# A first node pass with k and v only, beside the edge tables; q and skip inside the steps; no zero fills

## The chip, the cores and the metric

One core of a Trainium2 chip runs the whole kernel. The time is device microseconds of one launch. It is given as the median of several runs; the trace is of one further, profiled execution.

## The reference

The graph has 12500 nodes of 128 features (`x`) and 200000 edges. The edges are sorted by destination `dst`; the sources `src` are random. The destinations are not spread evenly: low node numbers have many more edges than high ones. Two residual blocks follow each other, each with a layer norm and a ReLU in front:

```
h = max(layernorm(x), 0)
x = x + conv2(conv1(h))              # two attention layers
h = max(layernorm(x), 0)
x = x + tensor_product_scatter(h)    # returned

conv(x):                             # 4 heads x 32
    q, k, v = x@Wq+bq, x@Wk+bk, x@Wv+bv
    e = edge_weight * We
    alpha = sum_c(q[dst] * (k[src]+e)) / sqrt(32)
    p = exp(alpha - segment_max(alpha, dst)[dst])
    w = p / segment_sum(p, dst)[dst]
    return segment_sum((v[src]+e) * w, dst) + x@Ws + bs

tensor_product_scatter(x):           # 32 scalars and 32 vectors a node
    s = tensor_product(x[src], edge_attr_9, w0..w4)
    return segment_sum(s, dst) / sqrt(10)
```

The term `x@Ws + bs` is called skip below.

## The kernel before

The nodes are cut into 98 windows of 128 nodes, the edges into 1563 tiles of 128, four tiles to a group: 391 groups. An edge that has a group's first destination plus 0 to 127 as its destination is a one of a 128x128 matrix (`O`, `one_hot`, L719), so that TensorE can bring a node's row to its edges and sum edges into their nodes.

*Edge tables* (`gnn_kernel`, from L1175). `dst`, `src` and `edge_weight` are loaded with one tile to a row and turned by TensorE, so that a tile becomes a column. Many small DMAs with strides fetch the first and last destination of the tiles and groups. A `flag` says whether the list meets the assumptions on its order (it does for this input); the program then branches on it (L1296) into `sorted_path`, else into `general_path`, which never runs here.

*Sorted path: tables and zero fills* (L556 to about L645). `REL` is each edge's destination relative to its group's first, `SEL` and `PEN` handle nodes that lie in two groups, `b_int` holds the groups' first nodes, the weights are joined to `WA` (q, an edge column per head, k, v: 388 columns). ScalarE's DMA queue writes zeros to all of `sum_d` (two tensors, named `fsum` in the trace) and `out_d` (`fout`) in DRAM.

*First node pass* (L690 to 705). 14 iterations of seven windows: load x, statistics on DVE, normalise with ReLU on ACT, and per window a transpose, a product of 388 columns (L667), its eviction on DVE (L668), a product of 128 columns for skip (L672) and its eviction (L701). SyncE's queue stores q (`fq`), k and v (`fkv`) and skip (`fs`).

*The two attention layers* (`conv`, L846 on). The loop's order is written by hand (`manual_schedule`), and it is straight-line code. Step s does, among others: SyncE fetches the 128 rows of q of group s+4 (`fetch_q`, L864) from a row that it reads from `b_int` into a register with a bounds check; GpSimd (POOL) issues four indirect gathers for group s+3 (`fetch_kv`, L725), 128 rows of 1 KB each; TensorE brings q to the edges (`query`, L885), DVE makes the scores (L932 to 935); for group m = s - 12, DVE makes the messages (L895, L896), TensorE sums them (`sum_up`, L915, L917), ACT evicts the sums (L920) and SyncE stores them (L923). Once in eight groups, a batch's running maximum is found by scans (L952, L955, L982). The lag of 12 groups is the reason why k and v of 16 groups are held (`bufs=LAG + 4`).

When a window's last group is summed (`window_steps`), the node work of the window follows in the later steps: `nodes_between` in layer 0 (mean, transpose, skip, residual, product with the next layer's `WA`, eviction L786, three stores) and `nodes_mixed` in layer 1 (second layer norm and a product with 352 columns). Windows 96 and 97 fall after the last group, at different steps, so one is worked on after the other.

*Scatter* (`load`, `sums`, L1115 on). Gathers of 1408-byte rows (`hg`, eight groups held), products with the edge numbers on ACT and DVE, sums on TensorE (L1147), eviction (L1150), store (L1151), and `nodes_out` adds the residual and writes the output. Only SyncE's order is by hand here; for the other engines the framework's scheduler decides.

Of the kernel before, what the change touches and what calls it, by code (L numbers as in the profile page):

```python
# [18 lines left out]
U = 4  # L19
UNROLL = 4  # L20
# [6 lines left out]
def general_path(ctx: ExitStack, tc: tile.TileContext, x, src, dst, edge_attr, edge_weight, conv1, conv2, tpw, out,  # L27
# [38 lines left out]
    X = cpool.tile([P, NW, D], F32, name="X")  # L66
# [284 lines left out]
    with tc.tile_pool(name="nrm2", bufs=1) as np_:  # L351
        layernorm_pass(np_.tile([P, NW, 2], F32, name="nrm2"), second)

# [10 lines left out]
    with ExitStack() as st:  # L364
# [5 lines left out]
        with tc.tile_pool(name="aprep", bufs=2) as ap_:  # L370
            d2 = ap_.tile([P, TP], F32, name="d2", bufs=1)
            d4 = ap_.tile([P, TP], F32, name="d4", bufs=1)
            for g in range(NG):
# [10 lines left out]
                for j0 in range(0, 9, 4):  # L384
                    n = min(4, 9 - j0)
                    pt = psum.tile([P, 4, P], F32, name="qd", bufs=2)
                    for j in range(j0, j0 + n):
                        nc.tensor.transpose(pt[:, j - j0, :], rows[:, :, j], ident)
                    if j0 == 0:
                        nc.scalar.copy(ea[:, 0:4, c], pt)  # L390
                    for j in range(j0, j0 + n):
                        if j in tmap:
                            for k in tmap[j]:
                                nc.vector.tensor_copy(ea[:, 4 + k, c], pt[:, j - j0, :])
                        elif j == 6:
                            nc.scalar.copy(d2[:, c], pt[:, j - j0, :])
                        elif j == 8:
                            nc.scalar.copy(d4[:, c], pt[:, j - j0, :])

            nc.vector.tensor_scalar(ea[:, 8, :], d2, 2.0 * r3, None, op0=OP.mult)  # L400
            nc.vector.tensor_scalar(d2, d2, -r3, None, op0=OP.mult)
            nc.vector.tensor_sub(ea[:, 4, :], d2, d4)
            nc.vector.tensor_add(ea[:, 12, :], d2, d4)
# [65 lines left out]
        with tc.For_i(0, NW, 1) as w:  # L469
# [11 lines left out]
            wi = X[:, ds(w, 1), :].rearrange("p a b -> p (a b)")  # L481
            nc.vector.tensor_add(wi, wi, py)

    nc.sync.dma_start(out[0:half * P, :].rearrange("(w p) d -> p w d", p=P), X[:, 0:half, :])
    nc.scalar.dma_start(out[half * P:(NW - 1) * P, :].rearrange("(w p) d -> p w d", p=P), X[:, half:NW - 1, :])
    nc.sync.dma_start(out[(NW - 1) * P:N, :], X[0:LASTN, NW - 1, :])
# [7 lines left out]
def window_steps(nw, ngr):  # L494


    return [math.ceil(ngr * math.sqrt((w + 1) / nw)) + 3 for w in range(nw)]


def sorted_path(ctx: ExitStack, tc: tile.TileContext, x, src, dst, edge_attr, edge_weight, conv1, conv2, tpw, out,  # L500
                srcI, dstF, ewF, FG, LG, seg_d):
# [7 lines left out]
    E = src.shape[0]  # L509
# [10 lines left out]
    KW = 7  # L520
    GE = U * P
    LF = seg_d.shape[1]
    SQ = 2 * BG + 1
    assert NW % KW == 0 and D == P
    scale = 1.0 / math.sqrt(C)
    r3, r10, avg = math.sqrt(1.0 / 3.0), math.sqrt(0.1), 1.0 / math.sqrt(10.0)
    n0, n1 = math.sqrt(1.0 / 64.0), math.sqrt(3.0 / 96.0)
    AHEAD = 4
    CHAIN = 4
# [4 lines left out]
    batch = lambda j: list(range(starts[j], starts[j] + sizes[j]))  # L534
    batch_of = [j for j in range(NB) for _ in range(sizes[j])]
    take = {}
    for w, g in enumerate(window_steps(NW, NGR)):
        take.setdefault(g, []).append(w)
    MIX = 352

    dram = ctx.enter_context(tc.tile_pool(name="fdram", bufs=1, space=bass.MemoryType.DRAM))
    kv_d = [dram.tile([NW * P, 2 * D], F32, name=f"fkv{i}") for i in range(2)]
    q_d = [dram.tile([NW * P + P, QD], F32, name=f"fq{i}") for i in range(2)]
    s1_d = dram.tile([NW * P, D], F32, name="fs1")
# [5 lines left out]
    rows_of = lambda t, a: t[a * P:(a + KW) * P, :].rearrange("(w p) c -> p w c", p=P)  # L550

    cp = ctx.enter_context(tc.tile_pool(name="fconst", bufs=1))
    ident = cp.tile([P, P], F32, name="fident")
    make_identity(nc, ident)
    ones = cp.tile([1, P], F32, name="fones")
    nc.vector.memset(ones, 1.0)  # L556
    eps = cp.tile([P, 1], F32, name="feps")
    nc.vector.memset(eps, EPS)


    REL = cp.tile([P, NGR, U], F32, name="fREL")
    nc.vector.tensor_sub(REL, dstF[:, 0:NGR * U].rearrange("p (g u) -> p g u", u=U),
                         FG[:, :, None].to_broadcast([P, NGR, U]))
    b_int = cp.tile([1, NGR], I32, name="fb")
    nc.vector.tensor_copy(b_int, FG[0:1, :])
    pidx = cp.tile([P, 1], F32, name="fpidx")
    nc.gpsimd.iota(pidx, pattern=[[0, 1]], base=0, channel_multiplier=1, allow_small_or_imprecise_dtypes=True)
    SEL = cp.tile([P, NGR], F32, name="fSEL")
    nc.vector.memset(SEL[:, 0:1], 0.0)
    nc.vector.tensor_sub(SEL[:, 1:NGR], FG[:, 1:NGR], FG[:, 0:NGR - 1])  # L570
    nc.vector.tensor_scalar(SEL[:, 1:NGR], SEL[:, 1:NGR], pidx, None, op0=OP.is_equal)

    PEN = cp.tile([1, NB, SQ], F32, name="fPEN")
    nc.vector.memset(PEN, -BIG)
    with tc.tile_pool(name="fpen", bufs=1) as pp:
        v = pp.tile([1, NGR, 2], F32, name="pf")
        nc.vector.memset(v, -BIG)
        nc.vector.tensor_sub(v[:, 1:NGR, 0], LG[0:1, 0:NGR - 1], FG[0:1, 1:NGR])
        nc.vector.tensor_scalar(v[:, 1:NGR, 0], v[:, 1:NGR, 0], BIG, None, op0=OP.mult)
        nc.vector.tensor_sub(v[:, 0:NGR, 1], FG[0:1, :], LG[0:1, :])  # L580
        nc.vector.tensor_scalar(v[:, 0:NGR, 1], v[:, 0:NGR, 1], BIG, None, op0=OP.mult)
        even = sizes.count(BG)
        nc.vector.tensor_copy(PEN[:, 0:even, 1:SQ], v[:, 0:even * BG, :].rearrange("o (b g) j -> o b (g j)", g=BG))
        for j in range(even, NB):
            n = sizes[j]
            nc.vector.tensor_copy(PEN[:, j, 1:1 + 2 * n], v[:, starts[j]:starts[j] + n, :].rearrange("o g j -> o (g j)"))

    EW = cp.tile([P, NGR * U, 2], F32, name="fEW")
    nc.vector.memset(EW[:, :, 0:1], 1.0)
    nc.vector.tensor_copy(EW[:, :, 1], ewF[:, 0:NGR * U])  # L590


    WA, BA, WS, BS, WE = [], [], [], [], []
    row = lambda b_: bass.AP(tensor=b_.tensor, offset=b_.offset, ap=[[0, P], [1, D]])
    wm = cp.tile([P, MIX], F32, name="fwm")
    with tc.tile_pool(name="fprep", bufs=1) as wp:
        zero = wp.tile([P, KW * SW], F32, name="zero")
        nc.vector.memset(zero, 0.0)
        for i in range(2):
            nc.scalar.dma_start(q_d[i][NW * P:NW * P + P, :], zero[:, 0:QD])  # L600
        for a in range(0, NW, KW):
            for i in range(2):
                nc.scalar.dma_start(rows_of(sum_d[i], a), zero.rearrange("p (w c) -> p w c", c=SW))
            nc.scalar.dma_start(rows_of(out_d, a), zero[:, 0:KW * D].rearrange("p (w c) -> p w c", c=D))
        for li, (Wq, bq, Wk, bk, Wv, bv, We, Ws, bs) in enumerate((conv1, conv2)):
            wa = cp.tile([P, AW], F32, name=f"fWA{li}")
            ba = cp.tile([P, AW], F32, name=f"fBA{li}")
            ws = cp.tile([P, D], F32, name=f"fWS{li}")
            bst = cp.tile([P, D], F32, name=f"fBS{li}")
            we = cp.tile([P, D], F32, name=f"fWE{li}")  # L610
            nc.sync.dma_start(we, row(We))
            for c0, w_, b_ in ((0, Wq, bq), (QD, Wk, bk), (QD + D, Wv, bv)):
                nc.sync.dma_start(wa[:, c0:c0 + D], w_)
                nc.sync.dma_start(ba[:, c0:c0 + D], row(b_))
            nc.sync.dma_start(ws, Ws)
            nc.sync.dma_start(bst, row(bs))
            for t in (wa, ba):
                nc.vector.tensor_scalar(t[:, 0:D], t[:, 0:D], scale, None, op0=OP.mult)
                tm = wp.tile([P, D], F32, name="tmw", bufs=2)
                nc.vector.tensor_mul(tm, t[:, 0:D], we)  # L620
                nc.vector.tensor_reduce(t[:, D:QD], tm.rearrange("p (h c) -> p h c", h=H), AX.X, OP.add)
            WA.append(wa)
            BA.append(ba)
            WS.append(ws)
            BS.append(bst)
            WE.append(we)

        w0 = wp.tile([32, 2, 32], F32, name="w0")
        nc.vector.memset(wm, 0.0)
        for j, (k, c0, f) in enumerate(((0, 0, n0), (1, 128, n1 * r3))):  # L630
            nc.sync.dma_start(w0[:, j, :], tpw[k].rearrange("u o w -> u (o w)"))
            nc.vector.tensor_scalar(wm[0:32, c0:c0 + 32], w0[:, j, :], f * avg, None, op0=OP.mult)
        w1 = wp.tile([P, 3, 3, 32], F32, name="w1")
        nc.vector.memset(w1, 0.0)
        for i in range(3):
            for k in range(3):
# [701 lines left out]
```

## Time and profile before

| | |
|---|---|
| median of 14 runs | 9321.29 us (9276.72 to 9351.28) |
| the profiled execution | 9316.81 us |
| its span, first to last instruction | 9315.0 us |
| mean granted TensorE clock | 0.764 |
| busy: PE / DVE / POOL / ACT | 63 / 54 / 48 / 19% |
| head, until the first gather | 0 to 272 us |
| attention layer 0 | 272 to 3263 us |
| attention layer 1 | 3263 to 6213 us |
| scatter and output | 6213 to 9315 us |

The span lies 1.8 us under the execution's own time. The busy times are averages over stages that are limited by different things, so each stage is to be read alone. In the rows below, a group of instructions is given as line, engine, operation, output<-input by the names in the program, shape, count, then busy time, the mean in ns of one, and the idle time of the engine just before them with what ended it. "remote" and "issue" are waits whose end the trace can't tie to an instruction, and in which nothing shown was waited for.

### The profile page before, as it was taken

The page shows a single profiled execution, that of the slowest core. Times are in us where ns is not written, and L with a number is a line of the kernel's source. Part 1 is how long each engine was busy: PE and PEld are TensorE (multiplying, and loading weights), DVE is VectorE, ACT ScalarE, POOL GpSimd, SP SyncE. Part 2 cuts the span into 40 slices and gives each one's busy share as a digit, 9 for nine tenths or more (in the row PEclk, how much of TensorE's full clock was granted, in tenths as well). Part 3 has the DMA queues.
Part 4 walks back from the last instruction along what each step waited for, and adds up shares of the span by engine and source line. Part 5 has one row for each costly group of instructions (what it writes and reads, how often), then busy time and mean ns, then how long its engine had stood idle before and what let it go on. Part 6 is the DMA issues. An engine that isn't in the chain of part 4 may idle for free.

```text
span 9315.0 us, 113271 instructions
## 1 busy us (share of the span) xinstructions
PE 5826.4 (63%) x33627; PEld 4837.3 (52%) x33628; DVE 5004.0 (54%) x11883; ACT 1751.6 (19%) x5162; POOL 4479.4 (48%) x4729
## 2 busy tenths in 40 slices
PE   4456666666666645666666666656767666666766
PEld 2344545545544434445444545436666556555666
DVE  5345555555555634555555555655555555554555
ACT  2111111111111111122222222221112111111111
POOL 0455555555454355555555545535444445444543
PEclk7677777777777767777777777868878778887778
DMA  7333333334344333333333334434344434433443
GB/s 217 110 95 100 103 106 107 109 109 115 107 115 116 101 91 96 100 103 106 106 103 108 107 109 113 120 101 111 106 107 109 110 105 114 109 106 106 116 113 95
DMA packets 838118, 1019.90 MB, mean 109 GB/s; under 512 B 138151, under 2 KB 651377, under 8 KB 837492
## 3 DMA queue, kind: packets, MB, share of 16 engines
q0 software_dynamic: 250240, 692.16, 27.1%
q1 hardware_dynamic: 545233, 300.14, 11.3%
q10 hardware_dynamic: 42019, 20.26, 0.8%
q8 instruction: 270, 4.42, 0.2%
q14 instruction: 356, 2.92, 0.1%
HBM read 826.93 MB, written 185.10 MB: 109 GB/s over the span
## 4 chain that ended last, share of the span: by engine, by line
PE 25%; another core or an unknown queue 18%; DVE 8%; issue 7%; ACT 3%; DMA 2%; POOL 1%; SPq 0%; DVEq 0%; ACTq 0%; POOLq 0%
PE pa L1147 13%; PE pa L917 4%; PE pq L885 2%; PE po L906 2%; ACT M L1125 1%; DVE O L719 1%; POOL kv L725 1%; PE pa L915 1%; DVE msg L895 1%; PE pa L1144 1%; DVE prod L932 1%; DVE top L952 1%; DVE tops L955 1%; DVE AL L935 1%
## 5 line engine op out<-in xcount | busy, mean ns | idle before, releaser
L725 POOL DMA_INDIRECT kv<-fkv,srcI x3128 | 2989.8, 956 | 2870.8 <-issue 813.6
L1147 PE MATMUL pa<-M,O 128*128 128x128 f32 (+1 forms) x12512 | 1926.1, 316 | 993.2 <-ACT acc L1150 759.2
L1147 PEld LDWEIGHTS pa<-M,O 128*128 128x128 f32 x12512 | 1784.6, 227 | 1148.6 <-ACT acc L1150 795.7
L725 POOL DMA_INDIRECT hg<-fhm,srcI x1564 | 1482.5, 948 | 1644.5 <-issue 1388.3
L906 PE MATMUL po<-fident,O 128*128 128x128 f32 x3128 | 677.3, 356 | 1316.8 <-DVE O L719 1075.0
L885 PE MATMUL pq<-qw,OT 128*128 128x132 f32 x6256 | 1091.6, 330 | 645.1 <-ACT OT L908 379.3
L917 PE MATMUL pa<-msg,O 128*128 128x136 f32 x6256 | 1433.3, 367 | 13.6 <-DVE msg L896 6.5
L885 PEld LDWEIGHTS pq<-qw,OT 128*128 128x128 f32 x6256 | 1007.4, 238 | 752.4 <-ACT OT L908 521.0
L917 PEld LDWEIGHTS pa<-msg,O 128*128 128x128 f32 x6256 | 1161.1, 256 | 288.1 <-issue 275.4
L906 PEld LDWEIGHTS po<-fident,O 128*128 128x128 f32 x3128 | 460.5, 180 | 1428.6 <-issue 819.3
L719 DVE TENSOR_TENSOR O<-iob,fREL 128x512 f32<-128x512 f32 x1173 | 799.7, 682 | 686.7 <-remote 414.3
L908 ACT COPY OT<-po 128x512 f32<-128x512 f32 x782 | 458.2, 586 | 2501.8 <-PE po L906 931.9
L932 DVE TENSOR_TENSOR prod<-pq,kv 128x512 f32<-128x512 f32 x782 | 534.3, 683 | 697.4 <-remote 287.9
L895 DVE TENSOR_TENSOR msg<-kv,wb 128x512 f32<-128x512 f32 x782 | 527.6, 675 | 276.1 <-ACT cfb L1004 224.7
L1150 ACT COPY acc<-pa 128x128 f32<-128x128 f32 x391 | 104.1, 266 | 2460.1 <-remote 1235.2
L935 DVE TENSOR_REDUCE AL<-prod 128x16 f32<-128x528 f32 x782 | 549.6, 703 | 26.8
L920 ACT COPY acc<-pa 128x136 f32<-128x136 f32 x782 | 213.6, 273 | 1593.1 <-PE pa L917 607.7
L1125 ACT ACTIVATE M<-hg,s 128x128 f32<-128x128 f32 x1564 | 505.8, 394 | 9.2 <-DMA hg<-fhm,srcI 7.9
L1129 DVE TENSOR_TENSOR M<-hg,sh 128x384 f32<-128x384 f32 x391 | 214.2, 548 | 455.9 <-remote 380.9
L1140 DVE TENSOR_TENSOR M<-M,tm 128x384 f32<-128x384 f32 x782 | 426.2, 545 | 0.2
L1139 DVE TENSOR_TENSOR tm<-hg,sh 128x384 f32<-128x384 f32 x782 | 405.8, 565 | 0.0
L915 PE MATMUL pa<-acc,fSEL 128*1 128x136 f32 x1368 | 334.7, 335 | 0.0
(184 smaller groups left out, 4236.4 us busy)
## 6 DMA issues: line engine op xcount, KB each, us to landing
fsum<-acc SPq DMA_DIRECT2D x782, 68.0 KB
qw<-fq SPq DMA_DIRECT2D x782, 66.0 KB
kv<-fkv,srcI POOLq DMA_INDIRECT x3128
hg<-fhm,srcI POOLq DMA_INDIRECT x1564
fout<-acc SPq DMA_DIRECT2D x391, 64.0 KB
fhm<-qkv SPq DMA_DIRECT2D x98, 176.0 KB
fsum<-zero ACTq DMA_DIRECT2D x28, 476.0 KB
A<-fsum SPq DMA_DIRECT2D x196, 68.0 KB
```

Source lines behind the costliest of these rows:

```text
L719: nc.vector.tensor_tensor(O, iob[:, None, :].to_broadcast([P, U, P]), REL[:, g, :, None].to_broadcast([P, U, P]), op=OP.is_equal)
L725: nc.gpsimd.indirect_dma_start(out=t[:, u, :], out_offset=None, in_=rows[:, :], in_offset=bass.IndirectOffsetOnAxis(ap=srcI[:, g * U + u:g ...
L885: nc.tensor.matmul(pqs[g][:, u, 0:QD], OT[:, u, :], qw, start=True, stop=True)
L895: nc.vector.tensor_mul(msg[:, :, :, 0:C], kv4(kv, D), pp[:, :, i, :, None].to_broadcast([P, U, H, C]))
L906: nc.tensor.transpose(po[:, u, :], Os[g][:, u, :], ident)
L908: nc.scalar.copy(OTs[g], po)
L915: nc.tensor.matmul(pa[0:1, :], SEL[:, g:g + 1], accs.pop(g - 1).rearrange("p h c -> p (h c)"), start=False, stop=False)
L917: nc.tensor.matmul(pa, O[:, u, :], msg[:, u].rearrange("p h c -> p (h c)"), start=(u == 0), stop=(u == U - 1))
L932: nc.vector.tensor_mul(prod[:, :, :, 0:C], pq[:, :, 0:D].rearrange("p u (h c) -> p u h c", h=H), kv4(kvs[g], 0))
L935: nc.vector.tensor_reduce(ALs[j][:, :, i, :], prod, AX.X, OP.add)
L1125: nc.scalar.activation(M[:, u, 0, :], hg[:, u, 0:P], AF.Copy, scale=s0[:, i * U + u:i * U + u + 1])
L1147: nc.tensor.matmul(pa[:, 0:n], O[:, u, :], M[:, u, c, 0:n], start=(u == 0 and c == 0), stop=(u == U - 1 and c == 2))
```

## The change

1. The first and last destinations of the groups come from TensorE (products with a selection matrix `pick` and with the identity) in place of the small strided DMAs. Casts go in blocks of four tiles, `REL` is made straight from PSUM, and the checks behind `flag` take fewer operations.
2. The zero fills go, except for the last window of the two `sum_d`. `window_steps` is clamped to the last group.
3. The first node pass moves ahead of the branch. It makes only k and v, from seven windows at a time. The normalisation is split: POOL subtracts the mean from all seven windows at once, ACT takes ReLU behind the transposes, and the factor 1/std goes into the evictions, four of them on DVE and three on ACT, with POOL adding the bias to the latter. The factors of all windows stay in `RS`. q and skip are made here for the first seven windows only.
4. Small table work (a list `beside`: `SEL`, `PEN`, weights, iota and so on) is put on POOL in between, some five pieces per iteration.
5. In layer 0, `nodes_asked` makes q and skip of the other 91 windows in the steps, two windows a batch, ahead of their use.
6. `bases` reads both row numbers of a step at once, from a table of pairs, without a bounds check.
7. The windows left at the last group are worked on at once, each in its own half of an idle `pq` bank, and the loop has three steps less.
8. More buffers: kv 16 -> 18 groups, hg and O in the scatter 8 -> 14, A, s1 and mv 2 -> 4, xt 4 -> 5, qkv, y and hT 2 -> 3. The scores' transpose tile `aT` shares one PSUM bank, `ab`, with the new asks.

`general_path` is changed too, but does not run.

```diff
-    return [math.ceil(ngr * math.sqrt((w + 1) / nw)) + 3 for w in range(nw)]
+    return [min(math.ceil(ngr * math.sqrt((w + 1) / nw)) + SLACK, ngr) for w in range(nw)]
+def query_steps(nw, ngr):
+    sizes, out, e = batch_sizes(ngr), [], -1
+    for n in sizes:
+        e += n
+        out += [e + 6, e + 8]
+    return {KW + k: s for k, s in enumerate(out[:nw - KW])}
...
-        for a in range(0, NW, KW):
-            for i in range(2):
-                nc.scalar.dma_start(rows_of(sum_d[i], a), zero.rearrange("p (w c) -> p w c", c=SW))
-            nc.scalar.dma_start(rows_of(out_d, a), zero[:, 0:KW * D].rearrange("p (w c) -> p w c", c=D))
+    for i in range(2):
+        nc.scalar.dma_start(window(sum_d[i], NW - 1), sh_.zero)
...
-    def base_of(g):
-        return nc.values_load(b_int[0:1, g:g + 1], engines=[SPE], min_val=0, max_val=N - 1)
+    def bases(*where):
+        _, v = nc.values_load_multi_w_load_instructions(
+            sh_.bases[0:1, where[0]:where[-1] + 1], engines=[SPE], min_val=0, max_val=N - 1,
+            skip_runtime_bounds_check_because=...)
+        return v
...
+    def nodes_asked(pool, nd, w):
+        st = {}
+        def load():
+            st["x"] = pool.tile([P, D], F32, name="xq", bufs=2)
+            load_x(st["x"], w)
+        def turn():
+            st["h"] = pool.tile([P, D], F32, name="hq", bufs=2)
+            nc.scalar.activation(st["h"], st["x"], AF.Relu, bias=sh_.RS[:, w, 1:2], scale=sh_.RS[:, w, 0:1])
+            nc.tensor.transpose(nd[:, 0:P], st["h"], ident)
+            st["hT"] = pool.tile([P, P], F32, name="hqT", bufs=2)
+            nc.scalar.copy(st["hT"], nd[:, 0:P])
+        def project():
+            nc.tensor.matmul(nd[:, 0:QD + D], st["hT"], sh_.WQ, start=True, stop=True)
+        def evict():
+            st["q"] = pool.tile([P, QD + D], F32, name="qs", bufs=2)
+            nc.vector.tensor_add(st["q"], nd[:, 0:QD + D], sh_.BQ)
+        def store():
+            nc.sync.dma_start(window(q_d[0], w), st["q"][:, 0:QD])
+            nc.sync.dma_start(window(s1_d, w), st["q"][:, QD:QD + D])
+        return [(-6, "load", load), (-2, "late", turn), (-1, "early", project), (-1, "late", evict), (0, "store", store)]
...
-            kvs[g] = pool.tile([P, U, 2 * D], F32, name="kv", bufs=LAG + 4)
+            kvs[g] = pool.tile([P, U, 2 * D], F32, name="kv", bufs=LAG + 6)
...
-            hg = pool.tile([P, U, MIX], F32, name="hg", bufs=8)
+            hg = pool.tile([P, U, MIX], F32, name="hg", bufs=14)
...
+                if m == NGR:
+                    spare = ps.tile([P, U, 256], F32, name="pq").rearrange("p (w u) c -> p w (u c)", w=2)
+                for k, w in enumerate(take.get(m, [])):
+                    for d, place, f in nodes(pool, nd if m < NGR else spare[:, k, :], w):
                         plan.setdefault((s + d, place), []).append(f)
-                if 0 <= m - 1 < NGR:
-                    store_sums(m - 1)
-                if 0 <= s + AHEAD < NGR:
-                    fetch_q(s + AHEAD)
+                run(s, "store")
+                q, r = s + AHEAD, m - 1
+                if 0 <= q < NGR and 0 <= r < NGR:
+                    bq, br = bases(2 * q, 2 * q + 1)
...
+                if 0 <= r < NGR:
+                    store_sums(r, br)
+                if 0 <= q < NGR:
+                    fetch_q(q, bq)
```

The new first node pass, in `gnn_kernel` ahead of the branch:

```diff
+        def normalized(a):
+            if a + 2 * KW < NW:
+                xs[a + 2 * KW] = load_x(a + 2 * KW)
+            xt = xs.pop(a)
...
+            for w in range(KW):
+                nc.vector.bn_stats(st[:, w, :], xt[:, w, :])
+                nc.vector.bn_aggr(mv[:, w, :], st[:, w, :])
+            nc.gpsimd.tensor_sub(xt, xt, mv[:, :, 0:1].to_broadcast([P, KW, D]))
+            rs = RS[:, a:a + KW, :]
+            nc.scalar.activation(rs[:, :, 0], mv[:, :, 1], AF.Sqrt, bias=eps)
+            nc.vector.reciprocal(rs[:, :, 0], rs[:, :, 0])
+            nc.vector.scalar_tensor_tensor(rs[:, :, 1], mv[:, :, 0], -1.0, rs[:, :, 0], op0=OP.mult, op1=OP.mult)
+            hT = npool.tile([P, KW, P], F32, name="hT", bufs=2) if a else hT0
+            for b, n in ((0, 4), (4, 3)):
+                pt = ps.tile([P, 4, P], F32, name="pt")
+                for k in range(n):
+                    nc.tensor.transpose(pt[:, k, :], xt[:, b + k, :], ident)
+                nc.scalar.activation(whole(hT[:, b:b + n, :]), whole(pt[:, 0:n, :]), AF.Relu)
+            return hT
+        def keys(a, hT):
+            kv = npool.tile([P, KW, 2 * D], F32, name="kvn", bufs=2)
+            for w in range(KW):
+                r = RS[:, a + w, 0:1]
+                pj = ps.tile([P, 2 * D], F32, name="pj", bufs=3)
+                nc.tensor.matmul(pj, hT[:, w, :], WKV, start=True, stop=True)
+                if w % 2:
+                    nc.scalar.activation(kv[:, w, :], pj, AF.Copy, scale=r)
+                else:
+                    nc.vector.scalar_tensor_tensor(kv[:, w, :], pj, r, BKV, op0=OP.mult, op1=OP.add)
+            nc.gpsimd.tensor_add(kv[:, 1:KW:2, :], kv[:, 1:KW:2, :], BKV[:, None, :].to_broadcast([P, KW // 2, 2 * D]))
+            nc.sync.dma_start(rows_of(kv_d[0], a), kv)
...
+            for a in range(0, NW + KW, KW):
+                hN = normalized(a) if a < NW else None
+                for f in beside[0:each]:
+                    f()
+                del beside[0:each]
+                if a:
+                    keys(a - KW, hT)
+                hT = hN
```

## The prediction

> **What bounds the kernel now.** I first cut the trace into its stages (boundaries read off the timeline: the first gather at 272, the next layer's first gather at 3263, the scatter's first work at 6213) and asked for each engine's busy time in them. Columns: stretch, length, busy us (instructions) of PE, PEld, DVE, ACT, POOL, then granted clock, DMA share, GB/s.
>
> ```profile
> core 0: us, PE busy (x) PEld busy (x) DVE busy (x) ACT busy (x) POOL busy (x), PEclk, DMA share, GB/s
> 60.00:130.00 70.00, 0.00 (x0) 0.00 (x0) 1.35 (x8) 1.28 (x1) 0.00 (x0) 0.50 0.96 274
> 130.00:272.00 142.00, 112.14 (x490) 72.61 (x490) 105.40 (x438) 64.66 (x210) 0.25 (x1) 0.94 0.75 222
> 272.00:3263.00 2991.00, 1828.26 (x9776) 1452.57 (x9776) 1616.48 (x3917) 423.94 (x1224) 1498.63 (x1564) 0.75 0.38 106
> 3263.00:6213.00 2950.00, 1788.81 (x9580) 1431.70 (x9580) 1606.12 (x4012) 669.94 (x1622) 1491.19 (x1564) 0.74 0.37 104
> 6213.00:9315.00 3102.00, 2086.73 (x13733) 1872.53 (x13733) 1639.45 (x3374) 577.09 (x2053) 1482.55 (x1564) 0.80 0.40 109
> ```
>
> From 60 to 130 no engine works and the DMA engines are 96% busy: that is the zero fills. SyncE's queue shows what the node pass's first load then waited for:
>
> ```profile
> SPq L682 <- DMA fout<-zero: 62.3, 1, 62.3
> ```
>
> From 130 to 272 the node pass runs, bound by no single engine (PE 79%, DVE 74%). In the three long stages no engine is over 68% busy. There I looked at the chain of waits and, in the timeline, at what stands still while POOL issues gathers one behind the other:
>
> ```profile
> PE 25%; another core or an unknown queue 18%; DVE 8%; issue 7%; ACT 3%; DMA 2%; POOL 1%; SPq 0%; DVEq 0%; ACTq 0%; POOLq 0%
> ...
> L725 POOL DMA_INDIRECT kv<-fkv,srcI x3128 | 2989.8, 956 | 2870.8 <-issue 813.6
> ```
> ```profile
> 304.85 0.95 POOL L725 DMA_INDIRECT kv<-fkv,srcI  x1 [0.30 <-issue]
> 305.44 0.69 DVE L932 TENSOR_TENSOR prod<-pq,kv 128x512 f32<-128x512 f32 x1 [19.33 <-remote]
> ```
> ```profile
> 316.70 0.59 ACT L908 COPY OT<-po 128x512 f32<-128x512 f32 x1 [29.65 <-remote]
> ```
>
> A gather takes 0.95 us and starts 0.30 us after the last: 1.25 us each, four to a step, 5.0 us a step. The step itself takes 2991 / 391 = 7.65. At the head of each layer 64 gathers run without a break (80 us), and only four steps are done in that time; DVE and ACT then stand still 19 and 30 us "for remote", a signal that comes late. So the long stages are bound by the chain DVE-PE-ACT of a step, stretched whenever POOL runs a burst. No part of the change removes a gather.
>
> **The change, part by part.**
>
> *Start (272 us before the first gather).* Removed: the 28 + 14 zero stores; the 70 us in which nothing else ran go. The new node pass has no wait on them and needs the flag no more, so it follows the edge tables. Its DVE work per iteration of seven windows, by these rows of the old pass:
>
> ```profile
> L667 PE MATMUL pj<-fWA,hT 128*128 128x388 f32 x196 | 86.6, 524 | 16.2 <-ACT hT L662 16.0
> L668 DVE TENSOR_TENSOR qkv<-pj,fBA 128x388 f32<-128x388 f32 x98 | 54.9, 560 | 27.8 <-PE pj L667 25.1
> ...
> L672 PE MATMUL pk<-fWS,hT 128*128 128x128 f32 x196 | 38.1, 277 | 0.0
> ...
> L701 DVE TENSOR_TENSOR s<-pk,fBS 128x128 f32<-128x128 f32 x98 | 27.4, 280 | 0.0
> L649 DVE BATCH_NORM_STATS2 st<-xt 128x6 f32<-128x128 f32 x98 | 24.6, 269 | 64.5 <-DMA xt<-in_x_dram 64.5
> ...
> L660 PE MATMUL pt<-fident,h 128*128 128x128 f32 x98 | 19.4, 279 | 96.4 <-ACT h L656 96.4
> L650 DVE BATCH_NORM_AGGREGATE mv<-st 128x2 f32<-128x6 f32 x98 | 14.8, 165 | 0.3
> ```
>
> Between 128 columns (0.280) and 388 (0.560) lies 1.08 ns a column, so a DVE eviction of 256 costs 0.42. Seven statistics 7 x 0.434 = 3.04, four evictions 1.68, two tiny operations 0.35: 5.07 us, x14 = 71 us. The other three evictions go to ACT. PE, from busy time per window, since its instructions overlap: a product is 86.6 / 98 = 0.88 at 388 columns and 38.1 / 98 = 0.39 at 128, so 0.63 at 256; with the transpose (19.4 / 98 = 0.20) 0.83, x98 = 81 us. DMA: 6.4 MB in, 12.8 MB out, at the 274 GB/s of the fill 70 us. So PE is the longest. DVE's edge work before that: 22.3 us were busy from 0 to 40 (the same view); casts in blocks of 512 and fewer checks leave about 17 (estimate). The first index rows arrive at about 8. The tail after the last iteration (products, evictions and store, q and skip of the first seven windows 7 x 0.42, the branch): 10. Sum 8 + 17 + 81 + 10 = 116. If DVE sets the pass it is 106; if PE is only 79% busy, as in the old pass, 8 + 17 + 81 / 0.79 + 10 = 138. I take 118, near the sum, since the loads run two iterations ahead. First gather 272 -> 118: **-154** (bounds 105 to 140: -167 to -132).
>
> One rule speaks against moving the subtraction and the addition (128x896 and 128x768) to POOL. The row first:
>
> ```profile
> 40.14 1.77 DVE L562 TENSOR_TENSOR fREL<-dstF,FG 128x1564 f32<-128x1564 f32 x1
> ...
> 40.55 2.28 POOL masks.py:199 TENSOR_SCALAR_AFFINE_SELECT fident<-fident 128x128 f32<-128x128 f32 x1
> ```
>
> The same select took 0.28 us at the kernel's head, with DVE free; here it took 2.0 longer. The Trainium skill ("SBUF — State Buffer", Who interferes with whom) says that the two engines share a port pair under an exclusive lock, and that a DVE instruction with two SBUF inputs holds up POOL instructions that read SBUF, while one with at most one SBUF input does not. By the lock, were each of POOL's two operations held 2.0 us, POOL's iteration would be at most 3.7 + 4.0 = 7.7 us against PE's 5.8, and the start 14 x 1.9 = 27 us later, -127 in place of -154. By the exception, nothing: the new evictions have one large operand in PSUM and the statistics have one input. I go with the exception; no row of the trace shows it. (POOL's 3.7 is a bound from above: 896 + 768 columns at the 2.2 ns of the select, 0.28 us for 128.)
>
> *Asks (q and skip of 91 windows inside layer 0's steps).* Per window ACT relu and copy (0.49 + 0.27), PE a transpose and a product (about 0.20 + 0.63), one DVE eviction of 260 columns (0.42), three SP DMAs. What a window's extra work costs in a step is read from two stretches of ten batches (80 steps) in layer 0, with 4 and with 32 windows of the between-layer pass in them (counted by their evictions L786):
>
> ```profile
> 480.17:1056.16 575.99, 340.82 (x1909) 274.13 (x1907) 294.17 (x657) 82.28 (x234) 304.40 (x319) 0.76 0.35 99
> 2473.65:3094.15 620.50, 391.07 (x2063) 308.91 (x2063) 359.60 (x918) 89.78 (x263) 308.12 (x320) 0.76 0.41 114
> ```
>
> (620.50 - 575.99) / 28 = 1.59 us a window; in that a window has 2.6 us of DVE work, two transfers of the PE-ACT chain and six DMAs. An ask has a sixth of the DVE work and about half of the PE-ACT part: I take half, 0.8 x 91 = **+73**. Bounds: 0 if it all falls into DVE's and PE's idle 40%; 2.4 each, its own chain 0.49 + 0.20 + 0.27 + 0.63 + 0.42 and two handovers of 0.2 in full, = +218.
>
> *Deeper buffers.* kv 16 -> 18 groups: two more groups, 8 more gathers, 10 us more in the opening burst of each layer; the last two steps then run without gathers, at the 4 us of the layers' last steps in place of 7.5, 7 back. Scatter 8 -> 14: 30 us more burst, 6 x (7.7 - 4.5) = 19 back. Sum 2 x 3 + 11 = **+17** (0 if steps run through the burst, +50 without any payback). In between POOL always waits for a free buffer, so depth changes nothing there.
>
> *SP.* One register load of two values and no bounds check per step: SP's rows shorten, but in the timeline qw is issued at least 18 us before its use and the sums are stored behind ACT. What hides it is this lead; so **0** (-40 to 0; with the cover gone a step would gain about 0.1 us). The two fq stores per batch now stand ahead of a qw fetch that must follow them; 2 to 3 us against the same 18: 0.
>
> *Last windows at once.* The last four follow one another at about 4.3 us each behind the layer's last sum (evictions at 3246.1, 3250.7, 3255.1, 3259.4); two side by side save about one: **-5** a layer, -10 (0 to -14).
>
> Sum on the profiled execution (9316.8, its span 9315.0): 9316.8 - 154 + 73 + 17 + 0 - 10 = 9242.8. The median of the runs lies 4.5 above it: **9247**.
>
> **The rivals.**
> *Asks on the chain (slower).* In a step already stretched by bursts each of the ask's three handovers may meet a late signal. The sum of the other terms is -147; the point from which it decides is (147 + 19) / 91 = 1.8 us an ask. At 2.4 it is 9316.8 - 147 + 218 + 4.5 = 9392. For it: "remote" is 18% of the chain. Against: whole windows with more handovers cost 1.59. A stretch of it (1.6 to 1.8) ends within 18 us of no change.
> *POOL holds the node pass.* If POOL's operations are slow, the 3.7 us with 2 us of waiting on each and five pieces of the `beside` work at 0.7 between them, 11.2 us an iteration against 5.8, that is 14 x 5.4 = 76 later: first gather at 194, 9323. That the start does not shrink as it says is this case; its 9323 is no change.
> *Steps gain (faster).* If shorter SP rows and deeper buffers smooth the bursts by 0.1 us a step in the layers and the scatter (1173 x 0.1 = 117), or the asks are hidden wholly: 9247 - 117 = 9130. For it: SP instructions take 0.70 us in a burst. Against: SP's lead.
>
> **How the numbers follow.** Forecast 0.62 (its own range 9170 to 9305); asks on the chain 0.14, POOL-bound pass 0.07, steps gain 0.17. The bulk of the forecast with the nearer part of the rivals makes 9130 to 9330. This kernel's measurement can tell about 0.2%, 19 us, from no change: faster than 9302 is forecast and steps gain, nearly whole, 0.79; within 9302 to 9340 the slow pass and the weakest asks, 0.08; above, 0.13.
>
> **What would show it.** First gather at 105 to 140; no stretch with all engines idle ahead of it. POOL's subtraction and addition at 1 to 2 us each, and DVE over 74% busy in the node pass. Layer 0 longer than before by 50 to 100 with layer 1 within 10. Opening bursts of 72 and 56 gathers. Wrong: the first gather past 150, or a layer-1 or scatter stage that moves by more than 30 either way, since nothing in its steps was priced.

## The result and the profile after

The changed kernel takes 22969.53 us (median of 10 runs, 22926.29 to 23026.15), the kernel before 9328.86 (47 runs): a ratio of 2.462, interval 2.4575 to 2.4667. The forecast was 9247 us.

The first line of the page of the changed kernel, and its largest groups of gathers, of products with the scores (`al`) and of the last stage's sums (lines left out are marked ...):

```profile
span 22909.1 us, 319824 instructions
...
L237 POOL DMA_INDIRECT kv<-kv_d,idx x3648 | 3447.6, 945 | 12850.8 <-DVE dd L243 10179.3
...
L282 PE MATMUL bb<-ident,al 128*128 128x128 f32 x29184 | 4790.0, 325 | 794.6 <-DVE al L272 792.4
L463 PE MATMUL qd<-O,M 128*128 128x128 f32 (+1 forms) x14592 | 3443.3, 403 | 2582.5 <-ACT M L446 1713.1
```

No line of `conv` or of the scatter is in the trace. Lines 237, 282 and 463 belong to `general_path`; its gathers read `kv_d` through a list `idx`, not `fkv` through `srcI`. The instructions rose from 113271 to 319824, and of the 12851 us that POOL stands idle before the gathers 10179 end with DVE (`dd`). The same is seen stage by stage (columns as before):

```profile
0.00:135.00 135.00, 94.62 (x408) 73.61 (x409) 83.27 (x334) 43.44 (x98) 75.73 (x82) 0.90 0.65 186
135.00:365.00 230.00, 115.10 (x323) 48.42 (x323) 160.35 (x669) 92.98 (x323) 2.64 (x6) 0.81 0.30 100
365.00:8690.00 8325.00, 5463.21 (x29772) 4455.25 (x29772) 3680.67 (x12696) 1010.12 (x2409) 1723.77 (x1824) 0.71 0.11 32
```

Up to 135 us the new edge tables and node pass run as the change describes. Then the program branches to `general_path`, which starts over with a pass of its own until its first gather at 365; the third row is its first attention layer, 8325 us alone.

So the flag was 1. The check that sets it (part 1 of the change; L1281 to 1285) asks that the first node `FG[g]` of each group g, from group 3 on, lies above a parabola:

```
t = (g * f - 3 * f)^2,  f = sqrt(98 * 128) / 391
bad[6] = max over g = 3..390 of (t - FG[g]) + 0.01
flag = max(bad) > 0
```

In this input the groups 0 to 3 all begin at node 0 (the first 2048 edges lead to nodes 0 and 1), and the parabola is 0 at group 3. Then t - FG is 0 there, and the margin of 0.01 alone makes the check fire. Worked out from the list, the other seven checks are at 0 or below. What the account of the change says of `general_path`, that it does not run, is therefore wrong of the changed kernel; it holds for the kernel before.

The experiments ran on chips 3, 5, 10 and 14 (the chip of the first profile is not recorded), and there the kernel before takes 6655 to 6670 us in place of 9329. Every ratio below is to the kernel before on the same chip in the same session. The changed kernel takes 22966 there (chip 14), as it did in the result.

### The profile page after: what moved, and what is told of

It is laid out like the page before. It is cut to its first block, busy times and chain, and to the rows that moved or that the text cites. A ratio compares the mean times of both kernels' runs of the same rounds, so it can differ in the third digit from the quotient of the medians.

```text
span 22909.1 us, 319824 instructions
## 1 busy us (share of the span) xinstructions
PE 14284.4 (62%) x75179; PEld 11674.2 (51%) x75180; DVE 9929.4 (43%) x33154; ACT 2909.9 (13%) x7368; POOL 5655.7 (25%) x5559
## 5 line engine op out<-in xcount | busy, mean ns | idle before, releaser
L237 POOL DMA_INDIRECT kv<-kv_d,idx x3648 | 3447.6, 945 | 12850.8 <-DVE dd L243 10179.3
L282 PEld LDWEIGHTS bb<-ident,al 128*128 128x128 f32 x29184 | 4631.4, 237 | 1567.0 <-DVE al L272 1435.9
L282 PE MATMUL bb<-ident,al 128*128 128x128 f32 x29184 | 4790.0, 325 | 794.6 <-DVE al L272 792.4
L463 PE MATMUL qd<-O,M 128*128 128x128 f32 (+1 forms) x14592 | 3443.3, 403 | 2582.5 <-ACT M L446 1713.1
L463 PEld LDWEIGHTS qd<-O,M 128*128 128x128 f32 (+1 forms) x14592 | 2743.6, 259 | 3267.6 <-ACT M L446 1909.1
L284 DVE TENSOR_REDUCE mt<-bb 128x4 f32<-128x1024 f32 x1824 | 2233.2, 1224 | 3002.6 <-PE bb L282 2241.2
L430 POOL DMA_INDIRECT hg<-h_d,idx x1824 | 2130.1, 1168 | 4290.7 <-DVE dd L434 3824.1
L266 PE MATMUL qd<-qw,OT 128*128 128x132 f32 x7296 | 1668.2, 384 | 838.1 <-issue 480.3
L266 PEld LDWEIGHTS qd<-qw,OT 128*128 128x128 f32 x7296 | 1351.8, 268 | 1075.1 <-issue 778.8
L279 PE MATMUL bb<-neg,identb 128*128 128x512 bf16 x3648 | 1689.8, 493 | 30.9
```

The source lines that it names most:

```text
L237: nc.gpsimd.indirect_dma_start(out=kv[:, u, :], out_offset=None, in_=kv_d[:, :], in_offset=bass.IndirectOffsetOnAxis(ap=idx[:, u:u + 1], a ...
L266: nc.tensor.matmul(pq[:, j, 0:QD], OT[:, g + j, :], qw, start=True, stop=True)
L279: nc.tensor.matmul(pb[:, j, :, :], identb, neg[:, u, None, :].to_broadcast([P, H, P]), start=True, stop=False)
L282: nc.tensor.matmul(pb[:, j, h, :], al[:, u, h:h + 1].to_broadcast([P, P]), ident, start=False, stop=(h == H - 1))
L284: nc.vector.tensor_reduce(mt[:, g // 2, :], pb.rearrange("p j h e -> p h j e"), AX.XY, OP.max)
L430: nc.gpsimd.indirect_dma_start(out=hg[:, u, :], out_offset=None, in_=h_d[:, :], in_offset=bass.IndirectOffsetOnAxis(ap=idx[:, u:u + 1], ax ...
```

## The experiments

**e1: the cause.** One check begins a group later; everything else of the change stays.

```diff
-        worst(6, t[:, 1, SLACK:NGR])
+        worst(6, t[:, 1, SLACK + 1:NGR])
```

> The changed kernel, with one of its eight order checks (the window check, number 6) begun one group later, so that group 3 is left out. Theory A: the changed kernel ran general_path because this check adds 0.01 to its worst value, and at group 3 the value is exactly 0 - 0 (the parabola starts at group 3, and the first node of group 3 is node 0 in this list). Then the flag is now 0, the sorted path runs, the trace has three long stages with lines of conv and the scatter again, and the time is that of the intended change: my terms give 9247 (9130 to 9330). Rival B: another check fires as well (order of the edges by the new TensorE products, or the check on q being asked in time): general_path runs again and the time stays at 22970 within 1%.

Measured: 6559.75 us against 6654.71, ratio 0.985 (0.9828 to 0.9874). The sorted path runs, so check 6 was the only one that fired: theory A, as far as the path goes. The intended change is worth 95 us on this chip, 1.5%. The 9247 itself can't be compared with it.

**e7: the margin alone.** Group 3 left in, the margin at 0.

```diff
-        nc.vector.tensor_scalar(bad[:, 6:7], bad[:, 6:7], 0.01, None, op0=OP.add)
+        nc.vector.tensor_scalar(bad[:, 6:7], bad[:, 6:7], 0.0, None, op0=OP.add)
```

> The changed kernel with the margin of check 6 at 0.0 in place of 0.01, group 3 left in. Theory A: at group 3 both the parabola and the first node are exactly 0, so the worst value is 0.0, the margin alone set the flag; the sorted path runs, 6540 to 6600. Rival: the two terms of the parabola do not cancel exactly on the engine, or another group is over the bound; then general_path runs, near 21500.

Measured: 6552.21 (one run) against 6660.94. The sorted path runs: no other group is over the bound, and at group 3 the parabola cancels exactly. It was the 0.01.

**e2, e9, e11: what the slow path costs.** The kernel before, made to take its own `general_path`; the changed kernel as it is; and e2 with the loops unrolled as in the changed one.

```diff
-        nc.vector.tensor_single_scalar(flag, bad[0:1, 1:2], 0.0, op=OP.is_gt)
+        nc.vector.tensor_single_scalar(flag, bad[0:1, 1:2], -BIG, op=OP.is_gt)
```
```diff
-UNROLL = 4
+UNROLL = 2
```

> The kernel before with its flag always 1, so that it runs its own general_path. Theory A: the cost of the changed kernel is general_path as such; then this takes 22500 to 23300, and the kernel before would have been as slow had its flag fired. Rival: the edits to general_path (loops unrolled twice instead of four times, x kept in DRAM) are a large part of 22970; then this takes clearly less, 15000 to 21000.

> The changed kernel as it is, on the chip of the experiments, to set against e2 (general_path of the kernel before, 21500). Theory A: the edits to general_path weigh little next to the path itself; 21200 to 21800 and a ratio to the kernel before of 3.2 to 3.3. Rival: unrolling by two and x in DRAM cost a few per cent: 22200 or more.

> e2 (general_path of the kernel before) with its pipelined loops unrolled by two instead of four, nothing else. Theory A: the 1466 us between general_path before (21500) and after (22966) come from the unrolling, in each of the three stages (571, 252 and 476 us); then this takes 22700 to 23000. Rival: they come from x being kept in DRAM and the work ahead of the path (head 171 us); then 21500 to 21900.

Measured: e2 21500.1 (ratio 3.229, 3.220 to 3.237), e9 22966.31 (3.447, 3.440 to 3.453), e11 22731.06 (3.413, 3.402 to 3.423). e2 lies between what its two theories expected, e9 meets its rival and e11 its theory A: the path as such is most of the time, but the changed kernel is 6.8% slower on it. Halving the unrolling goes with 1231 of those 1466 us. The first gather, at 274 us in e2 and at 445 in e9, gives 171. Of these, 92 come from the branch, taken at 43 us in e2 and at 135 in e9: the node pass of the sorted path is done ahead of it and then thrown away. The other 79 are not the change's. They lie between the branch and the first gather. This stretch is the second of the result's stages above (230 us); here it is in e9, e2 and e11:

```profile
135.00:445.00 310.00, 195.89 (x322) 76.82 (x322) 159.69 (x665) 92.97 (x323) 2.26 (x5) 0.51 0.22 74
43.00:274.00 231.00, 115.23 (x322) 48.52 (x322) 159.43 (x665) 94.28 (x325) 2.21 (x5) 0.80 0.30 93
43.00:354.00 311.00, 195.84 (x322) 76.73 (x322) 159.27 (x664) 94.22 (x325) 2.22 (x5) 0.50 0.22 69
```

The result's trace and e9 are of the same program, and yet the stretch takes 230 us in one, with PE 115 us busy at a granted clock of 0.81, and 310 in the other, with PE 196 us busy at 0.51. Why the clock differs is open. e2 has the short stretch and e11 the long one, so 80 of the 1231 us are not the unrolling's either, and 140 or so of the 1466 stay unexplained (estimates from these rows; x kept in DRAM was not tried alone). The changed kernel with unrolling by four was not run.

**e3: the kernel before on these chips.** Unchanged, for its trace.

> The kernel before, unchanged, for its trace on the chip of the experiments. Theory A (of my prediction): POOL's bursts of gathers hold up the other engines everywhere; then its trace has the same stages as the one shown, each shorter by the same factor, and 'remote' is again near 18% of the chain. Theory B: the hold-ups belong to the chip of the first profile; then 'remote' is gone from the chain here, the early steps of a layer run at the 5.0 us that four gathers of 1.25 us need, and the head until the first gather is unchanged, 265 to 280 us.

Measured: 6678.3 us (one run). Its stages, and its chain of waits:

```profile
0.00:272.00 272.00, 122.98 (x538) 80.91 (x539) 142.04 (x582) 80.80 (x263) 7.04 (x38) 0.79 0.76 216
272.00:2467.00 2195.00, 1596.78 (x9776) 1272.88 (x9776) 1607.98 (x3917) 425.67 (x1224) 1520.31 (x1564) 0.85 0.51 144
2467.00:4622.00 2155.00, 1583.22 (x9580) 1276.17 (x9580) 1597.98 (x4013) 676.69 (x1622) 1518.92 (x1564) 0.82 0.50 143
4622.00:6676.00 2054.00, 1860.18 (x13733) 1650.54 (x13733) 1628.15 (x3374) 603.39 (x2053) 1479.57 (x1564) 0.94 0.60 164
```
```profile
PE 29%; DVE 14%; DMA 8%; POOL 5%; issue 5%; ACT 2%; SPq 0%; DVEq 0%; ACTq 0%; POOLq 0%
```

The head is the same to 0.2 us (272). The three long stages are shorter by 27, 27 and 34%, and "another core or an unknown queue", 18% before, is gone. A step takes 5.1 us in the first half of layer 0 in place of 7.2: that is four gathers of 1.25. Theory B. What I took for the kernel's limit, bursts of gathers that hold up the other engines, belongs to the conditions of the first profile.

The stages of e1, in the same order:

```profile
0.00:144.00 144.00, 94.20 (x408) 74.20 (x409) 81.32 (x337) 44.15 (x97) 75.69 (x82) 0.89 0.63 186
144.00:2359.00 2215.00, 1617.48 (x10050) 1283.24 (x10051) 1640.12 (x4010) 484.45 (x1406) 1510.68 (x1565) 0.87 0.54 151
2359.00:4518.00 2159.00, 1603.55 (x9580) 1294.54 (x9579) 1598.69 (x4012) 676.69 (x1622) 1519.71 (x1564) 0.82 0.50 143
4518.00:6568.00 2050.00, 1847.53 (x13733) 1636.94 (x13733) 1629.22 (x3374) 619.45 (x2053) 1479.74 (x1564) 0.95 0.60 164
```

The head is 128 us shorter, layer 0 is 20 longer (274 more PE instructions: the asks), the rest moves by 4. (The two are from chips 5 and 3.)

**e6: the zero fills alone.** The kernel before without them, but for the last window.

```diff
-        for a in range(0, NW, KW):
-            for i in range(2):
-                nc.scalar.dma_start(rows_of(sum_d[i], a), zero.rearrange("p (w c) -> p w c", c=SW))
-            nc.scalar.dma_start(rows_of(out_d, a), zero[:, 0:KW * D].rearrange("p (w c) -> p w c", c=D))
+        for i in range(2):
+            nc.scalar.dma_start(sum_d[i][(NW - 1) * P:NW * P, :], zero[:, 0:SW])
```

> The kernel before with one part of the change alone: the zero fills left out but for the last window of the two sum_d. Theory A: the node pass stood behind them, so the first gather comes 60 to 72 us earlier and the time falls by the same. Theory B: the node pass then waits for its own loads and stores, as DMA was 96% busy, and less than 40 us is won.

Measured: ratio 0.9895 (0.9872 to 0.9918), 55 to 85 us; the first gather at 210.3 in place of 271.9, 61.6 earlier. The first gathers of e3 and e6 (both on chip 5):

```profile
271.94 1.10 POOL L725 DMA_INDIRECT kv<-fkv,srcI  x1 [0.62 <-DVE iob L711]
```
```profile
210.28 1.11 POOL L723 DMA_INDIRECT kv<-fkv,srcI  x1 [0.62 <-DVE iob L709]
```

Theory A. Half of the head's gain is the fills alone.

**e4: asks undone.** q and skip of all windows in the first pass. (This run and all that follow have e1's edit too.)

```diff
-    asks = {s: w for w, s in query_steps(NW, NGR).items()}
+    asks = {}
...
+                pj = ps.tile([P, QD + D], F32, name="pj", bufs=3)
+                nc.tensor.matmul(pj, hT[:, w, :], WQ, start=True, stop=True)
+                nc.vector.scalar_tensor_tensor(qs[:, w, :], pj, r, BQ, op0=OP.mult, op1=OP.add)
...
```

> The changed kernel with check 6 mended as in e1, and q and skip of all windows made in the first pass, none in the steps. Theory A (forecast): an ask costs 0.8 us in a step, 73 us in all, and 98 more products of 260 columns and evictions lengthen the first pass by 40 to 60 us; then layer 0 is 60 to 85 us shorter than in e1 and the whole 10 to 40 us shorter. Theory B: the steps are bound by POOL's gathers, the asks lie in the idle time of PE and DVE; then layer 0 is less than 20 us shorter and the whole 30 to 60 us longer than e1.

Measured: ratio 0.9826 (0.9808 to 0.9844), not to be told from e1. Layer 0 is 27.6 us shorter (2186.9 against 2214.5), the head 23.4 longer (167.8 against 144.4). e5, which has the asks and ran on e4's chip, gives 28.1 and 24.9. Neither theory: asks cost 27.6 / 91 = 0.30 us each, and q and skip in the first pass cost hardly less. The move into the steps gains nothing that these runs can tell.

**e5: old buffers.**

```diff
-            kvs[g] = pool.tile([P, U, 2 * D], F32, name="kv", bufs=LAG + 6)
+            kvs[g] = pool.tile([P, U, 2 * D], F32, name="kv", bufs=LAG + 4)
...
-            hg = pool.tile([P, U, MIX], F32, name="hg", bufs=14)
+            hg = pool.tile([P, U, MIX], F32, name="hg", bufs=8)
...
-            held[g] = hg, one_hot(pool, g, 14)
+            held[g] = hg, one_hot(pool, g, 8)
```

> The changed kernel with check 6 mended, and k/v of 16 groups, hg and O of 8 as before the change. Theory A (forecast): deeper buffers only lengthen the opening bursts, so this is 5 to 20 us faster than e1. Theory B: where gathers are the limit of the steps, depth does not matter, within 10 us. Theory C: depth keeps POOL busy over the stalls at batch ends; then this is 30 us or more slower than e1.

Measured: ratio 0.983 (0.9814 to 0.9845), overlapping e1's. The layers are the same to 1.1 us (2215.0 and 2158.1). The scatter took 2024, but with the deep buffers it took 2029 in e4 and 2050 in e1: theory B for the layers, and for the scatter nothing that can be told.

**e10: SP's row numbers.**

```diff
-        _, v = nc.values_load_multi_w_load_instructions(...)
-        return v
+        return [nc.values_load(sh_.bases[0:1, k:k + 1], engines=[SPE], min_val=0, max_val=N - 1) for k in where]
```

> e1 with one register load and a bounds check for each row number on SP, as in the kernel before. Theory A (forecast): SP's lead hides them, within 15 us of e1 (a ratio within 0.003 of its 0.985). Rival: SP's rows are on the path; 40 us or more slower than e1 (a ratio of 0.991 or more).

Measured: ratio 0.9845 (0.9831 to 0.9859). Theory A: the loads and checks cost nothing that can be told.

**e8 and e12: POOL's order in the node pass.** In e1 the pass took 100 us (first subtraction at 34.6, last addition begun at 134.2). Its group rows between 40 and 135 us:

```profile
L1404 POOL TENSOR_TENSOR kvn<-kvn,BKV 128x768 f32<-128x768 f32 x14 | 25.3, 1806 | 26.2 <-ACT kvn L1401 7.7 <-DVE st L1379 4.6 <-issue 4.5
L1381 POOL TENSOR_TENSOR xt<-xt,mv 128x896 f32<-128x896 f32 x13 | 21.9, 1687 | 0.5 <-DVE mv L1380 0.5
...
L1390 PE MATMUL pt<-fident,xt 128*128 128x128 f32 x91 | 16.2, 331 | 25.5 <-POOL xt L1381 25.5
```

The subtraction itself waits for almost nothing (0.5 us), but the addition ahead of it in POOL's queue waits 26 us, and PE's transposes then wait 25.5 us for the subtraction. e8 puts the addition of an iteration behind the next subtraction; e12 does the same in e4.

```diff
-            nc.gpsimd.tensor_add(kv[:, 1:KW:2, :], kv[:, 1:KW:2, :], ...)
-            nc.sync.dma_start(rows_of(kv_d[0], a), kv)
+            def bias():
+                nc.gpsimd.tensor_add(kv[:, 1:KW:2, :], kv[:, 1:KW:2, :], ...)
+                nc.sync.dma_start(rows_of(kv_d[0], a), kv)
+            return bias
...
                 hN = normalized(a) if a < NW else None
+                if owed:
+                    owed()
+                    owed = None
...
-                    keys(a - KW, hT)
+                    owed = keys(a - KW, hT)
...
```

> e1 with one order changed on POOL: the bias addition of an iteration comes after the mean subtraction of the next one, in place of before it. Theory A: the pass took 6.9 us an iteration in place of 5.8 because the subtraction stands in POOL's queue behind an addition that waits for ACT's evictions, so that PE's transposes start late (25.8 us of PE idle on it); then the first gather comes 15 to 30 us earlier, near 120, and the time falls by as much. Rival B: PE and POOL are bound by their own work (5.0 us and 3.5 to 8 us with the table work); then less than 8 us.

> e8 (check 6 mended, POOL's order changed) and e4 (q and skip of all windows in the first pass) in one. Theory A: asks cost about as much in the steps (28 us) as q and skip cost in the first pass (23 us), and POOL's order is worth 6 us in either; then a ratio of 0.979 to 0.984 to the kernel before, not to be told from e8's 0.982. Rival: with the asks gone POOL's order frees more, a ratio under 0.978.

Measured: e8 0.982 (0.9806 to 0.9834), first gather at 134.9 against 140.5 in e7 and e10 on the same chip: 5.6 us, rival B by the number. e12 0.9825 (0.9797 to 0.9853), theory A by the ratio, but its first gather, at 172.5, is no earlier than e4's 167.8 (on another chip). In e8 the wait halved (from 40 to 128 us):

```profile
L1390 PE MATMUL pt<-fident,xt 128*128 128x128 f32 x91 | 13.9, 293 | 12.3 <-POOL xt L1381 12.3
```

But another grew. In e1:

```profile
66.98 1.80 POOL L1404 TENSOR_TENSOR kvn<-kvn,BKV 128x768 f32<-128x768 f32 x1 [0.24 <-POOL pf L1328]
...
67.96 0.85 DVE L1385 SCALAR_TENSOR_TENSOR RS<-mv,RS 128x7 f32<-128x7 f32 x1
...
68.74 1.69 POOL L1381 TENSOR_TENSOR xt<-xt,mv 128x896 f32<-128x896 f32 x1
```

and in e8:

```profile
100.71 1.82 POOL L1405 TENSOR_TENSOR kvn<-kvn,BKV 128x768 f32<-128x768 f32 x1
100.73 1.82 DVE L1385 SCALAR_TENSOR_TENSOR RS<-mv,RS 128x7 f32<-128x7 f32 x1
```

A DVE instruction on 7 columns, 0.17 us at best, ends with POOL's addition: 0.85 us in the first case, 1.82 in the second. All 14 of them took 8.8 us in e1, 15.7 in e8, 15.9 in e4 and 22.4 in e12. DVE's queue behind it holds the next evictions. That this is why e8 won so little fits the numbers (6.9 us more on DVE), but no run took the conflict away. Nor does e8 show that engines were bound by their own work, as rival B has it: from 33 to 125 us POOL was 78% busy and PE 75%.

e8, at 6539.86 us, is below both kernels (6660.94 and 22966 on its chip). e4, e5 and e12 are not told apart from it.

## Why the prediction was wrong, point by point

*The failed step* is the path that runs behind the node pass. The prediction says of the new pass that it "needs the flag no more, so it follows the edge tables", and then prices all that follows as the sorted path. That the flag would still be 0 was taken over from the kernel before and not worked out. It was 1, and the program ran `general_path`, 22970 us in place of 9247. The change rewrites all of the flag's checks; I counted them only as "fewer checks", DVE time. The eight values can be worked out from the sorted list without a chip, and one is 0 + 0.01. Of the rivals, "that the start does not shrink as it says" stood for the change failing to do what it says; that the sorted path would not be reached at all was not among them, and the range had no room for 22970. e1 and e7 show the step by themselves.

*The terms*, for the path that was meant, on the chips of e1 and e3:

| term | forecast, us | measured, us | from |
|---|---|---|---|
| head | -154 (-167 to -132) | -127.5 to -131.5 | 271.9 (e3) to 144.4 (e1) and 140.4 (e10) |
| of it, zero fills | -70 | -61.6 | e6 |
| asks | +73 (0 to +218) | +28 | e1, e4: layer 0 |
| buffers | +17 | not told from 0 | e5 |
| SP | 0 | 0 | e10 |
| last windows at once | -10 (0 to -14) | +3.5 | e1, e3 |
| sum | -74 | -95 | e1, medians |

That the sum comes as near as it does is luck: the head and the last windows came out some 25 and 13 us worse than forecast, the asks and the buffers 45 and 17 better.

The head misses its bounds, by little. The edge work ends at 34.6 and not at 25: its DVE work is about as forecast (18 us), but its waits and the 11.7 us of PE products that make `FG` and `LG` were not priced. The pass does not need the flag, but its first statistics stand among the flag's checks in DVE's queue, so that its first subtraction starts right behind the flag:

```profile
34.56 1.69 POOL L1381 TENSOR_TENSOR xt<-xt,mv 128x896 f32<-128x896 f32 x1 [31.71 <-DVE flag L1298]
```

The pass took 100 us where PE's work was forecast at 81. PE's own work is below the forecast (70.9 us), POOL has 71.6 and DVE 59 (so 60% busy, not over 74%). I had taken the longest engine. That the pass is set by the loop over POOL, PE, ACT and back to POOL fits the waits in the rows above, but it is not shown: e8 cut one of these waits by half and won 5.6 us. The tail of 10 was about right (134.2 to 144.4).

The rule on the shared ports: POOL's 14 subtractions took 1677 to 1694 ns and its additions 1.8 us, within the bound of 3.7 for both, so POOL was not held up, as the exception of the Trainium skill has it for a DVE instruction with at most one SBUF input, outside the modes that use both of DVE's ports ("SBUF — State Buffer", Who interferes with whom). But I looked only at DVE's large instructions. The small one with two SBUF inputs meets the same rule from the other side: in the rows of e1 and e8 above it ends with POOL's addition.

The asks are mis-sized, 0.30 us each in place of 0.8, but this is on chips where a step has another limit, POOL's gathers; under the conditions of the first profile they were not measured. The last windows: from the last sum of a layer to the next gather it is 20.8 and 17.4 us in e3, 23.2 and 18.5 in e1, so the forecast 5 us a layer did not come; why was not tried.

*Right:* SP's loads at no cost, the fills' place on the path, layer 1 and scatter unmoved (4 us). None of it mattered to the result.

## What to carry to other kernels

Where a change touches the condition of a branch, work out the condition on the real data first: here one margin of 0.01 at an exact tie costs more than 13000 us, against some 100 us at stake in the path itself. After a run, look which functions' lines are in the page before any term is weighed. A loop over several engines in order can take longer than its busiest engine's work (here 100 us against 72), so its waits are to be priced too; an in-order queue that is shared by two steps of it (POOL's subtraction and addition) is a place to look for them, though mending this one won only 5.6 us. And where two runs of one program differ, compare the granted clock of the same stretch before a difference is put down to the code.

## What the runs showed of the hardware

The same program took 9321 us in the first runs and 6655 to 6670 on the four chips of the experiments, with the same head (272 us) and the same 0.95 us a gather; two things differ in the traces. "Remote" waits, in which other engines stand still during gathers, are 18% of the chain in the first profile (some 1680 us of its 9315) and none in e3. And the granted clock of the whole run was 0.764 against 0.867, PE's busy time for the same instructions 5826 us against 5163. What causes what is not shown. The changed kernel with `general_path` took the same in both, 22970 and 22966. Whether the chip or something else sets the first runs apart stays open, and so does what the mended change would bring there: it was not tried.

A DVE instruction of 0.17 us with two SBUF inputs took up to 2.13 us (e1) and 3.80 us (e8) beside POOL's long operations.

The granted clock of one stretch of `general_path` was 0.81 in one run and 0.51 in another run of the same program, and the stretch took 230 and 310 us.
